# Second attention of a two-layer model on one core: values of four heads in one step, long VectorE steps apart from one another, fronts begun earlier, stores issued later

## The chip, the cores and the metric

The kernel runs on one core of a Trainium2 chip. The metric is the time of one execution on the device in microseconds; of several runs the median counts. The profiler recorded one further execution, and all durations below are from that one.

## What is computed

The reference is a model of two layers over 16 x 512 = 8192 tokens of width 128, all in f32. Layer 0 (a recurrence, an attention and a ternary feed-forward) is not touched by the change. Layer 1 is `x + attention(xn) + experts(xn)`, with `xn` the normed `x`. Its attention has 16 heads of width 64. Queries see keys in a window of their own 128 positions and the 128 before, and besides 32 "global" keys, one for each segment of 16 positions, made by a softmax pooling of the segment. Cut to what matters:

```
q, kv  = rotary(x @ Wq) * SCALE, rotary(x @ Wkv)      # kv serves as keys and values
local  = layernorm(kv) of the block before and of this one
pkv    = softmax(segments(kv) @ Wproj)
glob   = layernorm(sum(segments(kv) * pkv))
sim    = [q . glob , q . local]  (masked)
attn   = softmax(sim);   o = attn @ [glob, local];   out = o @ Wout + bout
```

The experts take each token to one of 8 (the largest of a softmax, at most 1024 tokens each), run two matmuls with a relu between, and add the result scaled by the probability.

## The kernel before, in words

Layer 0 takes the first 5650 us of the span. Then comes the part named here the second stage. It handles 64 **units** of 128 positions (four to a sequence; t = 0 is the first of a sequence and has no block before it). A unit has four **groups** of four heads, so there are 256 groups, and the loop over `i` at the end of the kernel (lines 1477 to 1492) takes one group a turn.

Each group has three pieces, called by hand in this loop. `scores` (L1328) multiplies queries and keys into four PSUM tiles, has VectorE add the mask and take the maximum (L1350, written to `pr` and `am`) and ScalarE take the exponential (L1351). `weights_by_key` (L1359) transposes `pr` on TensorE in two halves of two heads each (tiles `pp`, L1373), and once per group the 32 global weights (`gp`, L1366), which VectorE copies to `gt` (L1368). `values` (L1378) multiplies the transposed weights with values into `o`; it too is called for two heads at a time. The loop runs `scores(i)`, then `weights_by_key(i-1, 0)`, `values(i-2, 0)`, `weights_by_key(i-1, 1)`, `values(i-2, 1)`. The tiles of `scores`, `gp` and `pp` share a ring of five PSUM buffers, so that each of them waits until the one five places ahead has been read. All else (projections, transposes of the fronts, experts) shares a ring of two, named `m_...`.

Between these pieces the loop calls `work(1)` six times a group (so 24 times a unit). `work` (L1446) walks through a list of generators, in a fixed order of rank, and runs each whose time has come up to its next `yield`. A `yield` with a positive n means "come back in n steps, and I have used this step's turn"; a negative one only sets the delay, and others may still run; 0 means "ask me again at the next step". The generators are

- `back(u)` (L1407), the end of unit u: the inverse of the softmax sum (`sum`, `rd`), stored and loaded again broadcast over partitions (`rb`), `ot = ot * rb` on GpSimd (L1430), the output projection `m_po` (L1435, L1436), a store to `r_d`.
- `front(u)` (L1159), the start of unit u: load `xu`, matmuls `m_kv` and `m_q`, rotary (GpSimd L1186 `raw`, L1189/1190 `kv`, L1208 `qt`), the norm's sums on VectorE (L1211 `hm`, L1213 `hd`, L1222 `hv`, L1234 `pl`) with `by_w` on GpSimd (L1217), the normed `n` (L1243) and its transposes (`m_nt`), pooling (`m_gp`), `gm`, `gd`, `gr`, then `lk` and `gv` on GpSimd (L1297 to L1304), and a store and loads that spread the global values into `gvb`.
- `routing()`: the router, then 64 scatters of tokens to the experts by GpSimd (`xe_d`), then 16 expert halves (`m_xep`, `m_hp`, `m_yp`).
- `results()` (L1127): after the experts, for each of 64 blocks a gather by GpSimd (`gy`), a load of `r_d`, the sum on VectorE (`res`, L1146) and the store of the output.

Each engine runs what it is given strictly in the order in which the program issues it; there is no scheduler behind. So the order is set by the loop, the ranks and the yields. A store or load stands in SyncE's queue, and one that waits holds those behind it. I name a place by group and step: 1.2 is the second `work` call in the second group of a unit (groups 0 to 3, steps 1 to 6).

Of the kernel before, what the change touches and what calls it, by code (L numbers as in the profile page):

```python
# [23 lines left out]
NT = T // P  # L24
# [45 lines left out]
def tile_kernel(  # L70
# [868 lines left out]
    with (  # L939
# [59 lines left out]
        def routing():  # L999
# [75 lines left out]
            xts = {}  # L1075
            for t in range(NT + 3):
                if t < NT:
                    xts[t] = wk.tile([P, D], F32, name=f"xts_{t}", tag="xts", bufs=4)
                    nc.sync.dma_start(xts[t], xt_d[t * P : (t + 1) * P, :])
                if t >= 3:  # L1080
                    nc.gpsimd.indirect_dma_start(
                        out=xe_d,
                        out_offset=bass.IndirectOffsetOnAxis(ap=slot[:, t - 3 : t - 2], axis=0),
                        in_=xts.pop(t - 3),
                        in_offset=None,
                    )
                yield -2
# [7 lines left out]
        def expert_half(e, hf):  # L1095
# [10 lines left out]
            nc.sync.dma_start(xe, xe_d[at : at + S, :].rearrange("(t p) d -> p t d", p=P))  # L1106
            yield -3
            ps = misc(f"xep_{nm}")
# [6 lines left out]
            for f in range(4):  # L1115
                hp = misc(f"hp_{nm}_{f}")
                mm(hp, w1_sb[:, f * P : (f + 1) * P], xeT)
                nc.scalar.activation(he[:, f, :], hp, AF.Relu)
                yield 1 + f // 3
            yp = misc(f"yp_{nm}")  # L1120
# [8 lines left out]
        def results():  # L1129

            while not experts_done[0]:
                yield 0
            for t in range(NT):
                while stored[0] <= t:
                    yield 0
                gy = wk.tile([P, D], F32, name=f"gy_{t}", tag="gy", bufs=3)
                nc.gpsimd.indirect_dma_start(
                    out=gy,
                    out_offset=None,
                    in_=ye_d,  # L1140
                    in_offset=bass.IndirectOffsetOnAxis(ap=slot[:, t : t + 1], axis=0),
                )
# [3 lines left out]
                nc.vector.scalar_tensor_tensor(res, gy, pk[:, t : t + 1], res, ALU.mult, ALU.add)  # L1146
                nc.sync.dma_start(out[t * P : (t + 1) * P, :], res)

# [6 lines left out]
        units, groups = {}, {}  # L1155

        def front(u):

            U = units[u] = Unit()  # L1159
            U.normed = False  # L1160
# [28 lines left out]
            nc.gpsimd.tensor_tensor(k[:, :, 0, :], c_[:, :, 0, :], s_[:, :, 1, :], ALU.subtract)  # L1189
            nc.gpsimd.tensor_tensor(k[:, :, 1, :], c_[:, :, 1, :], s_[:, :, 0, :], ALU.add)  # L1190
            U.qt = wk.tile([P, NHP, P], F32, name=f"qt_{u}", tag="qt", bufs=3)
            for c in range(2):
# [15 lines left out]
                nc.gpsimd.tensor_tensor(U.qt[:, 4 * c : 4 * c + 4, :], parts[0], parts[1], ALU.add)  # L1208
# [4 lines left out]
            nc.vector.scalar_tensor_tensor(  # L1213
# [39 lines left out]
            nc.vector.reciprocal(ss, ss)  # L1253
            nc.gpsimd.tensor_tensor(se, se, ss.unsqueeze(2).broadcast_to(shape), ALU.mult)
            U.lk = lks[u % 4]
            for c in range(2):
                ps = misc(f"nt_{u}_{c}")
# [69 lines left out]
        def scores(i):  # L1327
# [26 lines left out]
            G.pg = wk.tile([P, 4, NSEG], F32, name=f"pg_{i}", tag="pg", bufs=2)  # L1354
            nc.scalar.copy(G.pg, pr[:, :, W:KW])
            if g == 3:
                streams.insert(0, [back(u), tick[0] + 2])

# [18 lines left out]

        def values(i, two):  # L1378

            u, g = divmod(i, 4)  # L1380
            U, G = units[u], groups[i]
            b, t = divmod(u, TB)
            w = 2 * (g % 2) + two
            if w == 0:
                U.o = ps_o.tile([P, 4, P], F32, name=f"o_{i}", tag="o")
            o = U.o[:, w, :]
            mm(o, gvbs[b % 2][:, g, 2 * two : 2 * two + 2, :].rearrange("p a d -> p (a d)"), G.gt, True, False)
            before = [u - 1, u] if t else [u]
            for c, k in enumerate(before):
                for a in range(2):  # L1390
                    mm(
                        o[64 * a : 64 * a + 64, :],
                        lks[k % 4][:, 4 * g + 2 * two + a, :],
                        G.pts[two][:, a, c, :],
                        False,
                        c == len(before) - 1,
                    )
            if two == 1:
                del groups[i]
            if w < 3:  # L1400
# [4 lines left out]
            U.done = g == 3  # L1405

        def back(u):  # L1407
# [3 lines left out]
            nc.vector.reciprocal(U.sum, U.sum)  # L1411
            yield -2
# [4 lines left out]
            yield 2  # L1417
            nc.sync.dma_start(rd_d[u % 2], rd)
# [11 lines left out]
            nc.gpsimd.tensor_tensor(U.ot, U.ot, rb, ALU.mult)  # L1430
            yield -4
            po = misc(f"po_{u}")
# [4 lines left out]
            nc.vector.tensor_tensor(res, po[:, 0:D], bout_row, ALU.add)  # L1437
            yield 2
            nc.sync.dma_start(r_d[u * P : (u + 1) * P, :], res)
# [3 lines left out]
        streams = []  # L1443
        tick = [0]

        def work(n):  # L1446

            for st in list(streams):
                if st[1] <= tick[0]:
# [8 lines left out]
            tick[0] += 1  # L1458

        NU = NT  # L1460
# [140 lines left out]
```

## Time and profile before

| what | value |
|---|---|
| median of 3 runs | 7826.6 us (7825.79 to 7835.86) |
| the profiled execution's own time | 7828.71 us |
| its span, first to last instruction | 7826.9 us |
| busy share of the span | PE 90%, DVE 61%, ACT 59%, POOL 38% |
| granted TensorE clock, mean | 0.938 of full speed |
| second stage in the span | from 5651.8 us (first `m_kv`) to the end |
| first and last `ot` product (L1430) | 5741.4 and 7814.1 us |

PE is TensorE, DVE VectorE, ACT ScalarE, POOL GpSimd, SP SyncE. In a row of groups the columns are: line, engine, operation, names of output and inputs, shapes, how often; after the bar busy time in us and the mean of one in ns; after the second bar the engine's idle time ahead of them and what ended it. A row of the timeline has the start in us, the duration in us, engine, line, operation, names, shapes and how many instructions were merged; an idle time in front of it stands in brackets. Each f32 matmul leaves two matmul records, transposes leave one. A matmul's form is the part of the array that it uses: 128*64 has a stationary operand of 64 columns, half the array's width.

The starts of the 64 `ot` products give the length of each unit. They fall in four stretches, by what runs besides fronts, groups and backs:

| units (intervals between `ot` products) | beside them | us per unit |
|---|---|---|
| 2 to 10 | scatters, 7 a unit | 33.4 |
| 11 to 26 | experts, one half a unit | 36.2 |
| 27 to 36 | gathers, 4 to 5 a unit | 35.6 |
| 37 to 59 | gathers, 1 a unit | 30.2 |

### The profile page before, as it was taken

What the parts mean: (1) busy time and instruction counts of PE and PEld (TensorE: products, weight loads), DVE (VectorE), ACT (ScalarE), POOL (GpSimd) and SP (SyncE); (2) the same over time, 40 slices, a digit from 0 to 9 for tenths busy, and PEclk for the clock granted to TensorE, in tenths of its full rate; (3) what the DMA queues carried; (4) which work ended last, traced back from release to release, by engine and by line L of the source; (5) the groups of instructions that cost most, each with busy time, mean ns of one, the idle gap of its engine ahead of it and who ended that gap; (6) DMA issues with size and microseconds to landing.
All of it is one profiled execution on the core that took longest, in us unless ns stands there. A gap on an engine that the chain in (4) does not pass through costs nothing. (4 is left out here: it accounts for less than half of the span.)

```text
span 7826.9 us, 107889 instructions
## 1 busy us (share of the span) xinstructions
PE 7010.5 (90%) x38168; PEld 3230.2 (41%) x38168; DVE 4782.5 (61%) x9622; ACT 4616.3 (59%) x9357; POOL 3012.6 (38%) x3763
## 2 busy tenths in 40 slices
PE   6898999999999999999999999999678999889898
PEld 2233333333333333333333333333256666666666
DVE  4565666566666666666666666666266555666665
ACT  3565655566555666656666666656355666556666
POOL 3333332232323233222222222222268655667775
PEclk7999999999999999999999999999789999989999
DMA  2221222212222221122211222222211111111111
GB/s 70 80 81 66 74 69 66 85 62 68 69 71 69 70 66 65 63 67 70 71 60 62 69 79 71 81 74 88 83 28 52 51 41 46 42 44 34 33 35 36
DMA packets 394780, 492.23 MB, mean 63 GB/s; under 512 B 82304, under 2 KB 278016, under 8 KB 393088
## 3 DMA queue, kind: packets, MB, share of 16 engines
q1 hardware_dynamic: 390144, 476.94, 19.5%
q0 software_dynamic: 4096, 8.40, 0.4%
q8 instruction: 302, 4.95, 0.3%
q14 instruction: 238, 1.95, 0.1%
HBM read 348.87 MB, written 133.17 MB: 62 GB/s over the span
## 5 line engine op out<-in xcount | busy, mean ns | idle before, releaser
L915 DVE TENSOR_REDUCE nm<-n 128x1 f32<-128x512 f32 x4096 | 2587.5, 682 | 1479.6 <-PE n L177 1477.9
L917 ACT ACTIVATE pt<-t 128x512 f32<-128x512 f32 x4096 | 2216.3, 595 | 1882.1 <-PE t L177 1857.4
L177 PE MATMUL n<-kt,qt 72*128 72x512 bf16 x4096 | 1323.5, 389 | 203.5 <-DVE nm L915 158.9
L177 PE MATMUL t<-qt,kt 75*128 75x512 bf16 x4096 | 1357.9, 391 | 104.1 <-ACT pt L917 56.0
L177 PE MATMUL o<-pt,vt 128*32 128x512 f32 x8192 | 1123.0, 671 | 0.0
L177 PEld LDWEIGHTS <-qt 72*128 72x128 bf16 x4096 | 354.7, 98 | 1026.3 <-issue 881.9
L177 PEld LDWEIGHTS <-kt 75*128 75x128 bf16 x4096 | 399.9, 99 | 849.8 <-issue 519.8
L1351 ACT ACTIVATE pr<-pr,am 128x288 f32<-128x288 f32 (+1 forms) x1024 | 508.0, 498 | 209.8 <-DVE am L1350 209.2
L867 POOL CAST nmp<-nm 128x16 bf16<-128x16 f32 x256 | 50.0, 195 | 1451.3 <-DVE nm L915 1451.3
L177 PEld LDWEIGHTS o<-pt,vt 128*32 128x32 f32 x8192 | 231.0, 118 | 661.1 <-issue 526.0
L467 POOL TENSOR_TENSOR qk<-qk,parts 128x512 f32<-128x512 f32 x128 | 147.9, 1155 | 769.3 <-ACT parts L280 739.7
L1350 DVE CUSTOM_DVE_ANT_0 pr<-s,cst 128x288 f32<-128x288 f32 (+1 forms) x1024 | 372.6, 419 | 44.5 <-PE s L994 44.1
L1373 PE MATMUL pp<-ident,pr 128*128 128x128 f32 x1792 | 311.5, 294 | 94.5 <-DVE am L1350 93.6
L994 PE MATMUL o<-pt,lk 128*64 128x128 f32 x3584 | 327.3, 300 | 0.0
L1375 ACT COPY pt<-pp 128x512 f32<-128x512 f32 (+1 forms) x512 | 264.9, 526 | 97.4 <-PE pp L1373 95.8
L1200 DVE TENSOR_TENSOR q<-m_q,cst 128x512 f32<-128x512 f32 x256 | 177.1, 692 | 220.1 <-PE m_q L994 220.1
L994 PE MATMUL s<-lkt,qt 64*128 64x288 f32 (+1 forms) x2048 | 298.3, 408 | 0.4 <-ACT lkt L1317 0.4
L177 PE MATMUL m_in<-x,w 128*128 128x512 f32 x512 | 279.6, 632 | 17.9 <-POOL x L330 9.7
L1373 PEld LDWEIGHTS pp<-ident,pr 128*128 128x128 f32 x1792 | 214.8, 148 | 162.9 <-DVE am L1350 130.2
L994 PE MATMUL m_q<-xu,wq_sb 128*128 128x128 f32 x2048 | 278.5, 279 | 1.9 <-ACT raw L1183 0.8
L177 PE MATMUL m_f<-n,w 128*128 128x512 f32 x512 | 274.0, 618 | 2.9 <-POOL n L330 2.6
L994 PEld LDWEIGHTS m_q<-xu,wq_sb 128*128 128x128 f32 x2048 | 249.4, 192 | 20.1 <-ACT raw L1183 16.0
(333 smaller groups left out, 11104.7 us busy)
## 6 DMA issues: line engine op xcount, KB each, us to landing
qt<-q_d SPq DMA_DIRECT2D x768, 96.0 KB
kt<-k_d SPq DMA_DIRECT2D x256, 288.0 KB
rb_n<-rstd_d SPq DMA_DIRECT2D x64, 512.0 KB
rb<-rd SPq DMA_DIRECT2D x128, 256.0 KB
q_d<-parts SPq DMA_DIRECT2D x64, 384.0 KB
k_d<-parts SPq DMA_DIRECT2D x64, 384.0 KB
o_d<-og SPq DMA_DIRECT2D x512, 36.0 KB
oa<-o_d SPq DMA_DIRECT2D x64, 256.0 KB
```

The costliest lines, as they stand in the source:

```text
L177: nc.tensor.matmul(out, lhsT=lhsT, rhs=rhs, start=first, stop=last)
L467: nc.gpsimd.tensor_tensor(x, x, parts[:, 0], ALU.subtract)
L867: nc.gpsimd.tensor_copy(parts[:, 0], nm)
L915: nc.vector.tensor_reduce(dst, n, AX.X, ALU.max, negate=True)
L917: nc.scalar.activation(dst, n, AF.Exp)
L994: nc.tensor.matmul(out, lhsT=lhsT, rhs=rhs, start=first, stop=last)
L1200: nc.vector.tensor_tensor(q, ps.rearrange("p (i t) -> p i t", t=P), const(name)[:, t * P : (t + 1) * P].unsqueeze(1).broadcast_to([P, 4, P ...
L1350: nc.vector.tensor_tensor_reduce(pr[:, j, 0:n], s[:, 0:n], mask(t), -1.0, BIG, ALU.add, ALU.min, nmax)
L1351: nc.scalar.activation(pr[:, j, 0:n], pr[:, j, 0:n], AF.Exp, bias=nmax, scale=-1.0, accum_out=U.sum[:, 4 * g + j : 4 * g + j + 1])
L1373: nc.tensor.transpose(pp[:, a, c, :], G.pr[:, 2 * two + a, at : at + P], ident)
L1375: nc.scalar.copy(pt[:, :, 0:n, :], pp[:, :, 0:n, :])
```

## The change

1. `values` is called once a group for all four heads, right after `scores`; and the product with the global weights `gt`, which was one matmul of 128 columns for two heads, becomes two of 64 columns each.
2. The front is pulled apart: `hm` and `hd`, `n` and the sums stand in steps of their own; a helper `quiet` keeps the front's long VectorE steps out of the last two steps of a group. The two waits for the previous front (`normed`, and a new `weighed`) stand before parts of the front instead of at its start; two counters, `scored` and `valued`, hold it back where buffers would be lacking.
3. A front begins two groups earlier (twelve steps).
4. Delays grow: a unit's `rd` store, the `m_po` product after `ot`, the `r_d` store, the store and loads of the global values, the loads of the experts' input, and the store of the output after `res`. The scatter of a block follows its load after two turns instead of three.

The six `work` calls of a group stay, in other places. No operation is taken out; 512 matmuls are added (two of 64 columns for each one of 128).

```diff
-            for t in range(NT + 3):
+            for t in range(NT + 2):
...
-                if t >= 3:
+                if t >= 2:
...
             xe = wk.tile([P, TB, D], F32, name=f"xe_{nm}", tag="x3", bufs=1)
             nc.sync.dma_start(xe, xe_d[at : at + S, :].rearrange("(t p) d -> p t d", p=P))
-            yield -3
+            yield -5
...
-                yield 1 + f // 3
+                yield 1 + f // 3 * 2
...
                 nc.vector.scalar_tensor_tensor(res, gy, pk[:, t : t + 1], res, ALU.mult, ALU.add)
+                yield -4
                 nc.sync.dma_start(out[t * P : (t + 1) * P, :], res)
...
+        def quiet():
+
+            while phase[0] in (4, 5):
+                yield 0
+
         def front(u):
...
-            while u - 1 in units and not units[u - 1].normed:
-                yield 0
             x = wk.tile([P, P], F32, name=f"xu_{u}", tag="xu", bufs=3)
             nc.sync.dma_start(x, x3_d[b][:, t * P : (t + 1) * P])
-            yield -3
+            yield -5
+
+            while u - 1 in units and not units[u - 1].weighed:
+                yield 0
...
+            while scored[0] < u - 2:
+                yield 0
             U.qt = wk.tile([P, NHP, P], F32, name=f"qt_{u}", tag="qt", bufs=3)
...
             yield -1
+            yield from quiet()
             mean = wk.tile([P, H1], F32, name=f"hm_{u}", tag="hm")
             nc.vector.tensor_reduce(mean, kv, AX.X, ALU.add)
+            yield -1
+            while u - 1 in units and not units[u - 1].normed:
+                yield 0
+            yield from quiet()
             d = wk.tile(heads, F32, name=f"hd_{u}", tag="hd", bufs=1)
...
             yield -2
+            yield from quiet()
             var = wk.tile([P, H1], F32, name=f"hv_{u}", tag="hv")
...
+            yield -1
+            yield from quiet()
             pl = wk.tile([P, H1], F32, name=f"pl_{u}", tag="pl")
             nc.vector.tensor_reduce(pl, by_w, AX.X, ALU.add)
-            yield -4
+            U.weighed = True
+            yield -2
...
-            n = wk.tile(heads, F32, name=f"n_{u}", tag="hq", bufs=1)
-            nc.vector.tensor_tensor(n, d, rstd.unsqueeze(2).broadcast_to(heads), ALU.mult)
...
             nc.scalar.activation(se, se, AF.Exp)
+            yield 1
+            yield from quiet()
+            n = wk.tile(heads, F32, name=f"n_{u}", tag="hq", bufs=1)
+            nc.vector.tensor_tensor(n, d, rstd.unsqueeze(2).broadcast_to(heads), ALU.mult)
             U.normed = True
-            yield 2
...
+            while valued[0] < u - 2:
+                yield 0
             lk = U.lk
...
             yield -5
-            nc.sync.dma_start(gv_d[u % 2], gv[:, 0, :])
             ps = misc(f"gkt_{u}")
...
             yield -2
+            nc.sync.dma_start(gv_d[u % 2], gv[:, 0, :])
+            yield -4
             src = gv_d[u % 2].rearrange("(g j s) d -> j s g d", j=4, s=n_seg)
...
-                streams.insert(0, [back(u), tick[0] + 2])
+                streams.insert(0, [back(u), tick[0] + 3])
...
-        def values(i, two):
+        def values(i):
...
-            mm(o, gvbs[b % 2][:, g, 2 * two : 2 * two + 2, :].rearrange("p a d -> p (a d)"), G.gt, True, False)
...
+            for two in range(2):
+                o = U.o[:, 2 * (g % 2) + two, :]
+                for c, k in enumerate([None] + blocks):
+                    for a in range(2):
+                        if k is None:
+                            v, w = gvbs[b % 2][:, g, 2 * two + a, :], G.gt
+                        else:
+                            v, w = lks[k % 4][:, 4 * g + 2 * two + a, :], G.pts[two][:, a, c - 1, :]
+                        mm(o[64 * a : 64 * a + 64, :], v, w, c == 0, c == len(blocks))
...
             nc.gpsimd.tensor_tensor(U.ot, U.ot, rb, ALU.mult)
-            yield -4
+            yield -6
...
-            if i % 4 == 0 and begun[0] < NU:
+            if (i == 0 or i % 4 == 2) and begun[0] < NU:
                 begin()
...
                 scores(i)
+                phase[0] = 0
                 work(1)
+            if i >= 2:
+                values(i - 2)
+            work(1)
             for two in range(2):
                 if 0 <= i - 1 < NG1:
                     weights_by_key(i - 1, two)
-                    work(1)
-                if i >= 2:
-                    values(i - 2, two)
-                    work(1)
+                work(1)
+            work(1)
             work(1)
```

Left out are the counters' own lines, the delays of `back` (2 to 3, 2 to 5, 2 to 5) and unchanged code.

More of the change, by code (lines that the diff above doesn't have):

```diff
@@ L1079, in routing @@
                     nc.sync.dma_start(xts[t], xt_d[t * P : (t + 1) * P, :])
-                if t >= 3:
+                if t >= 2:
                     nc.gpsimd.indirect_dma_start(
                         out=xe_d,
-                        out_offset=bass.IndirectOffsetOnAxis(ap=slot[:, t - 3 : t - 2], axis=0),
-                        in_=xts.pop(t - 3),
+                        out_offset=bass.IndirectOffsetOnAxis(ap=slot[:, t - 2 : t - 1], axis=0),
+                        in_=xts.pop(t - 2),
                         in_offset=None,
@@ L1155, in tile_kernel @@
         units, groups = {}, {}
+        def quiet():
+            while phase[0] in (4, 5):
+                yield 0
         def front(u):
             U = units[u] = Unit()
-            U.normed = False
+            U.normed = U.weighed = False
             b, t = divmod(u, TB)
-            while u - 1 in units and not units[u - 1].normed:
-                yield 0
             x = wk.tile([P, P], F32, name=f"xu_{u}", tag="xu", bufs=3)
             nc.sync.dma_start(x, x3_d[b][:, t * P : (t + 1) * P])
-            yield -3
+            yield -5
+            while u - 1 in units and not units[u - 1].weighed:
+                yield 0
             pair = [P, H1, 2, 32]
@@ L1255, in front @@
             U.lk = lks[u % 4]
+            yield -2
             for c in range(2):
@@ L1355, in scores @@
             nc.scalar.copy(G.pg, pr[:, :, W:KW])
+            scored[0] += g == 3
             if g == 3:
-                streams.insert(0, [back(u), tick[0] + 2])
+                streams.insert(0, [back(u), tick[0] + 3])
         def weights_by_key(i, two):
@@ L1376, in weights_by_key @@
             G.pts.append(pt)
-        def values(i, two):
+        def values(i):
             u, g = divmod(i, 4)
-            U, G = units[u], groups[i]
+            U, G = units[u], groups.pop(i)
             b, t = divmod(u, TB)
-            w = 2 * (g % 2) + two
-            if w == 0:
+            if g % 2 == 0:
                 U.o = ps_o.tile([P, 4, P], F32, name=f"o_{i}", tag="o")
-            o = U.o[:, w, :]
-            mm(o, gvbs[b % 2][:, g, 2 * two : 2 * two + 2, :].rearrange("p a d -> p (a d)"), G.gt, True, False)
[L1388 to L1400, printed above, removed]
+            blocks = [u - 1, u] if t else [u]
+            for two in range(2):
[7 more added lines that the diff above has]
+                        mm(o[64 * a : 64 * a + 64, :], v, w, c == 0, c == len(blocks))
+            if g % 2 == 0:
                 return
@@ L1405, in values @@
             U.done = g == 3
+            valued[0] += U.done
         def back(u):
@@ L1411, in back @@
             nc.vector.reciprocal(U.sum, U.sum)
-            yield -2
+            yield -3
             ps = misc(f"rd_{u}")
@@ L1416, in back @@
             nc.vector.tensor_copy(rd, ps[0:H1, 0:P])
-            yield 2
+            yield 5
             nc.sync.dma_start(rd_d[u % 2], rd)
@@ L1437, in back @@
             nc.vector.tensor_tensor(res, po[:, 0:D], bout_row, ALU.add)
-            yield 2
+            yield 5
             nc.sync.dma_start(r_d[u * P : (u + 1) * P, :], res)
@@ L1444, in tile_kernel @@
         tick = [0]
+        scored = [0]
+        valued = [0]
+        phase = [0]
         def work(n):
@@ L1458, in work @@
             tick[0] += 1
+            phase[0] += 1
         NU = NT
```

## The prediction

> **What bounds the kernel now.** I read the busy shares by stretch first, then TensorE's waits over the second stage, then the timelines of PE, DVE and POOL. Only the second stage changes. Rows by stretch (start:end, length, busy us of PE, PEld, DVE, ACT, POOL, then clock, DMA share, GB/s):
>
> ```profile
> 7100.00:7700.00 600.00, 540.89 (x4650) 405.81 (x4650) 400.20 (x1190) 384.59 (x1150) 432.13 (x395) 0.95 0.13 34
> 6302.00:6592.00 290.00, 272.90 (x2228) 199.59 (x2228) 165.81 (x483) 177.98 (x505) 165.21 (x153) 0.99 0.17 45
> 5888.00:6157.00 269.00, 228.74 (x1919) 170.14 (x1919) 164.24 (x474) 158.76 (x470) 213.13 (x200) 0.94 0.19 52
> ```
>
> With experts PE is busy 94% at a clock of 0.99; with scatters POOL reaches 79%; in the plain stretch PE has 90% at 0.95. No engine is full everywhere. What PE waits for, 5700 us to the end (total us, times, longest):
>
> ```profile
> PE pp L1373 <- DVE am L1350: 93.6, 48, 6.8
> PE m_po L994 <- POOL ot L1430: 66.7, 56, 3.8
> PE o L994 <- DMA gvb<-gv: 33.3, 8, 5.2
> ```
>
> So PE waits 265 us in all, mostly for VectorE to read the scores (whose PSUM buffers `pp` takes over) and for GpSimd's `ot`.
>
> **Values.** Four heads before: one half of `values`, then what follows; a unit's first block has two half-width matmuls less:
>
> ```profile
> 7444.49 0.39 PE L994 MATMUL o<-gt,gvb 128*128 128x128 f32 x2
> 7444.81 0.66 PE L994 MATMUL o<-pt,lk 128*64 128x128 f32 x8
> 7445.40 1.16 PE L994 MATMUL m_q<-xu,wq_sb 128*128 128x128 f32 x8
> ...
> 5706.71 0.44 PE L994 MATMUL o<-pt,lk 128*64 128x128 f32 x4
> 5707.08 2.05 PE L994 MATMUL m_q<-xu,wq_sb 128*128 128x128 f32 x16
> ```
>
> From start to next start: 0.32 us for the full matmul, 0.59 for four halves, 0.37 for two. Two more halves thus cost 0.22, as much as a full one (`m_q`: 0.90 for four, 0.22 each); the remaining 0.10 ahead and 0.15 behind is the change of width. Two calls cost 2 x 0.91 = 1.81 us a group. After: 12 halves, 6 x 0.215, and one change of width, 0.24: 1.53 us. The Trainium skill, TensorEngine Tiling (Array Packing), Key Properties, says that a change of tiling mode, though not of the tile, drains TensorE; that agrees in sign with the 0.25. The same page, Instruction Overhead, speaks against the change: each matmul costs some 60 cycles however small, so splitting a full one buys nothing by itself. By it alone (a half priced as a full one, 0.22) the step would be 12 x 0.22 + 0.24 = 2.9 us, 1.1 us dearer a group; the row of two more halves for 0.22 denies that, since halves of different columns overlap. Bounds: 1.45 (no change of width counted) to 1.75 (12 x 0.146, the mean of four halves). I take 1.53, by the marginal row: 1.1 us less PE a unit. Adding up a unit's rows (scores 1.17, half of `pp` 0.44, `m_q` 0.95, `m_kv` 0.96, `m_po` 2.1 and so on) PE needs 25.8 us before and 24.8 after for t > 0, 5.2 less for t = 0; an expert half adds 8.3 (0.6 + 4 x 1.0 + 3.7).
>
> **Waits that go.** `values` now stands between `scores` and `pp`, giving VectorE 1.5 us more, and no long front step is right ahead of `scores`: the 93.6 us and the slow clock after them I count as gone. The load of `gvb` gets some 6 us instead of 1: the 33.3 go. What is late next is GpSimd.
>
> **Where GpSimd's queue is moved.** In the changed issue order a unit's GpSimd work runs `gr`, `lk` (0.2), `qt`, `gd`, `gv`, `qt` (0.5), a gather or scatter (0.5), `by_w` (1.2), `ot` (1.4), and `m_po` comes at 2.4. Before, `raw` and both `kv` stood where now the second `qt`, a gather or scatter and `by_w` stand ahead of `ot`, and `m_po` was late by only 0.7 to 1.4 us. These rows bear on it (POOL, DVE, PE):
>
> ```profile
> 7453.73 2.26 POOL L1208 TENSOR_TENSOR qt<-q,q 128x512 f32<-128x512 f32 x1
> ...
> 6734.97 2.35 POOL L1430 TENSOR_TENSOR ot<-ot,rb 128x1024 f32<-128x1024 f32 x1
> ...
> 6749.34 1.03 POOL L1137 DMA_INDIRECT gy<-ye_d,slot  x1 [0.15 <-issue]
> ```
> ```profile
> 7453.53 1.33 DVE L1213 SCALAR_TENSOR_TENSOR hd<-hm,kv 128x1024 f32<-128x1024 f32 x1
> ...
> 6735.49 1.98 DVE L1146 SCALAR_TENSOR_TENSOR res<-gy,pk,res 128x128 f32<-128x128 f32 x1
> ...
> 6752.05 0.35 DVE L1146 SCALAR_TENSOR_TENSOR res<-gy,pk,res 128x128 f32<-128x128 f32 x1 [1.61 <-DMA gy<-ye_d,slot]
> ```
> ```profile
> 6740.31 0.77 PE L994 MATMUL o<-gt,gvb 128*128 128x128 f32 x2 [5.15 <-DMA gvb<-gv]
> ```
>
> `qt` takes 1.23 alone and 2.26 beside `hd`; `res` takes 0.34 alone and 1.98 beside `ot`, ending as `ot` ends. So the two exclude each other. The skill, GPSIMD Engine Reference, Specifications, only says that VectorE instructions with two SBUF inputs contend with GpSimd for the interfaces; by that rule without the row I would have charged nothing definite, by the row it is the whole overlap, 1.2 us a unit for `hd`. A gather lands 2.7 us after its start (6749.34 to 6752.05). After the 5.15 us idle PE ran at half speed for four groups of rows: 0.69, 1.06, 0.90 and 2.53 us against 0.32, 0.59, 0.44 and 1.89, 1.9 us lost.
>
> **Units with gathers** (28 of them with two, since `results` now waits 3 + 4 steps a block and is last in rank; before, 4 to 5 a unit in ten units and then one). From the start of group 0's scores: scores 1.17, `rd` 0.15, values 1.53, `m_gp` 0.58: 3.43. `gr` starts 1.5 later (7438.86 to 7440.36): 4.9. Then 0.86 + 2.31 + 1.23 + 0.85 + 1.23 + 1.2 (`hd`): 12.6; the gather starts at 12.8 and lands at 15.5, `by_w` holds the port until 16.3, `res` (placed at 1.2 in VectorE's queue) ends at 16.6, `gt` of this unit's group 0 behind it at 16.85. Queued behind `res` are that `gt`, `hv`, and the maxima of group 2. PE by its own rows reaches group 2's third score matmul, whose buffer that `gt` frees, at 3.43 + 0.55 + 0.95 + 0.44 + 0.95 + 1.17 + 1.53 + 0.55 + 0.17 + 0.44 + 0.57 = 10.75. It waits 6.1 us. From there to the unit's end: 0.58 + 1.53 + 0.55 + 0.17 + 0.44 + 2.1 + 0.96 + 1.17 + 0.96 + 5.6 = 14.1. Sum 30.9, with 2.0 for the clock and 0.3 for gaps 33.2; t = 0 saves 2.9; mean 32.5. Bounds of this wait: 4.5 us if `res` is not late and only `ot` (done at 18.5, `m_po` due at 14.0) is, about 8 if `pl` and `m_plt` come late too.
>
> **Units with experts.** Experts' matmuls now stand at 0.5 to 2.2, in the very stretch in which PE would wait: `m_po` is due at 14.0 + 8.3 = 22.3, `ot` is done at 12.6 + 2.35 + 2.33 = 17.3. PE bounds: 24.8 + 8.3 + 0.8 (a wait for `he`'s buffer, gaps) = 33.9 to 34.2, t = 0 29.5: mean 33.0 against 36.2. This is the gain; its cover gone (a scarcer PE cover, `he` late by one more step), it costs up to 1 us a unit.
>
> **Units with scatters.** Two scatters lie ahead of `by_w` (1.2, and 2.5 with its wait for the one before, as in rows of 1.5 us idle): `ot` ends at 21.0, PE waits 7.0, then 10.8 to the end: 31.8 + 2.3 = 34.1, t = 0 32.2: 33.7 against 33.4.
>
> **Other edits.** Stores issued later are covered by buffers that have a group to spare; what each would cost uncovered is one landing, some 2 us. `xu` and the experts' inputs are loaded two steps sooner: nothing. `rb` is now issued one step before `ot`, but SyncE isn't held by steps: `rd` is copied at 2.4, two landings later, by 8, `rb` is there, and `ot` is due at 16: nothing. SyncE's `out` store waits for `res` and holds `xu` and `gvb` behind it until 16.6; these are needed at 25: nothing. Filling: group 0's scores now stand behind the second front's transposes (5697.7 instead of 5684.5), but the third front's projections are done by then: +5, between -10 and +20.
>
> **Sum**, first to last `ot`, 2072.7 us before. After: first two units 75, 10 x 33.7 = 337, 17 x 33.0 = 561, 28 x 32.5 = 910, 3 x 32.5 = 98, last three 63: 2044, thus -29; with filling -24. From the profiled execution's 7828.7: 7805; the median lies 2.1 below: 7803.
>
> **Rivals.**
> *The gather's wait decides (slower).* Place: `res` at 1.2 on VectorE, behind a gather behind six GpSimd steps, in 28 units. Price as above 6.1 us; each further us a unit costs 28. It turns the sign at 32.5 + 24/28 = 33.4 us a unit. For it: the units with gathers before took 35.6, with a 5.15 us idle among them; against: they had twice the gathers. At 35.0: 7873.
> *GpSimd keeps ahead (much faster).* If `lk` or the gather slip in between, only `ot` is late: 31.0 a unit with gathers and 32 with scatters: 7803 - 28 x 1.5 - 10 x 1.7 = 7744. For it: `gr` might be ready earlier; against: the queue is strict and its rows are steady.
> *The change does not do what it says.* If halves don't overlap so well (1.75), three of four `values` lie on the path of each unit: 64 x 0.66 = +42: 7845.
>
> **Numbers.** A measurement of this kernel tells 0.2% (16 us) from no change. My likeliest case, 0.42, has its own range 7770 to 7835 and is split: 0.22 faster, 0.17 within, 0.03 slower. GpSimd ahead: 0.25, faster. The gather's wait: 0.25, of it 0.22 slower. Halves: 0.08, slower. So faster 0.47, within 0.20, slower 0.33. Two in ten are left out by 7720 to 7880.
>
> **What would show it.** Right: expert units at 33, a group of `o` rows in 1.5 us, no `pp` waiting for `am`; in units with gathers one idle of 6 us on PE in group 2, ended by `gt` or `am`, with `res` waiting for `gy` on VectorE. Wrong: `m_po` or nothing waiting there; expert units still at 36; an idle elsewhere, at `m_plt` or `m_nt`.

## The result and the profile after

The changed kernel takes 7932.7 us (median of 4 runs, 7924.4 to 7939.5) against 7826.2 us of before (4 runs): ratio 1.0132, 95% interval 1.0119 to 1.0145. It is slower by 106 us, where 7803 us had been forecast, and outside the forecast's 7720 to 7880 us. The profiled execution took 7929.1 us with a span of 7927.1 us at a granted TensorE clock of 0.929. The difference lies wholly in the second stage.

Unit lengths, measured as before by the starts of the `ot` products:

| intervals between `ot` products | beside them | forecast, us per unit | measured |
|---|---|---|---|
| first `ot` | | at 5746 | at 5746.9 |
| 0 and 1 | | 75 in all | 75.2 in all |
| 2 to 11 | scatters | 33.7 | 35.0 |
| 12 to 28 | experts | 33.0 | 34.2 |
| 29 to 56 | two gathers a unit | 32.5 | 35.5 |
| 57 to 59 | one gather a unit | 32.5 | 34.9 |
| the last three | | 63 in all | 63.3 in all |

10 x 1.3 + 17 x 1.2 + 28 x 3.0 + 3 x 2.4 is 125 us: that is the whole miss, 7929 less 7805. Two thirds of it lie in the units with gathers. The busy time by stretch, scatters, experts and two gathers (columns as before: PE, PEld, DVE, ACT, POOL, then the clock, DMA share, GB/s):

```profile
5822.00:6172.00 350.00, 269.39 (x2444) 208.48 (x2445) 194.65 (x582) 189.81 (x571) 263.99 (x248) 0.91 0.17 47
6230.00:6753.00 523.00, 483.34 (x4494) 367.93 (x4493) 317.50 (x918) 334.85 (x965) 319.88 (x295) 1.00 0.18 47
6754.00:7746.00 992.00, 742.54 (x7000) 577.14 (x7000) 644.89 (x1709) 542.39 (x1624) 636.59 (x588) 0.87 0.13 35
```

With gathers TensorE is busy 75% of the stretch at a clock of 0.87; in the plain units of before it was 90% at 0.95. What it waits for over the second stage, and what VectorE's `res` waits for:

```profile
PE s L994 <- DVE gt L1391: 209.8, 33, 7.1
PE m_gkt L1330 <- POOL gv L1325: 66.3, 45, 5.7
PE m_plt L1257 <- DVE pl L1250: 50.1, 14, 5.5
PE m_q L994 <- DVE sw L1296: 46.0, 59, 0.8
PE m_hp L994 <- ACT he L1118: 14.7, 13, 1.4
...
PE o L994 <- DMA gvb<-gv: 9.3, 9, 1.5
PE m_po L994 <- POOL ot L1449: 8.2, 7, 6.6
...
DVE res L1146 <- DMA gy<-ye_d,slot: 136.6, 32, 5.2
```

The old waits are gone or small: `pp` for `am` from 93.6 to 2.4 us, `m_po` for `ot` from 66.7 to 8.2, `o` for `gvb` from 33.3 to 9.3. A new one stands at the very place that the prediction named, TensorE's third score matmul of group 2 behind `gt`, in all 28 units with two gathers: 180.7 of the 209.8 us are theirs.

The values step, four heads at once, is even a little cheaper than forecast, 1.46 us from 7520.16 to 7521.62:

```profile
7520.16 0.44 PE L994 MATMUL o<-gt,gvb 128*64 128x128 f32 x4
7520.43 0.61 PE L994 MATMUL o<-pt,lk 128*64 128x128 f32 x8
7520.86 0.39 PE L994 MATMUL o<-gt,gvb 128*64 128x128 f32 x4
7521.08 0.61 PE L994 MATMUL o<-pt,lk 128*64 128x128 f32 x8
7521.62 0.65 PE L994 MATMUL m_gp<-kv,sw 128*32 128x64 f32 x32
```

The same unit around its gather, the rows of POOL, then DVE, then PE:

```profile
7531.38 1.10 POOL L1137 DMA_INDIRECT gy<-ye_d,slot  x1 [0.16 <-issue]
7532.51 2.34 POOL L1230 TENSOR_TENSOR by_w<-kv,rows_sb 128x1024 f32<-128x1024 f32 x1
7534.81 2.33 POOL L1449 TENSOR_TENSOR ot<-ot,rb 128x1024 f32<-128x1024 f32 x1
...
7533.99 3.32 DVE L1146 SCALAR_TENSOR_TENSOR res<-gy,pk,res 128x128 f32<-128x128 f32 x1 [4.70 <-DMA gy<-ye_d,slot]
7537.23 0.28 DVE L1391 COPY gt<-gp 128x128 f32<-128x128 f32 x1
...
7537.56 0.91 PE L994 MATMUL s<-lkt,qt 64*128 64x160 f32 x4 [5.43 <-DVE gt L1391]
```

The gather lands 2.6 us after its start (2.7 had been forecast), and `res` begins in the middle of `by_w`. But `res` does not end with `by_w` at 7534.85. It goes on until `ot` ends: 7533.99 + 3.32 = 7537.31, against 7537.14. A step of 0.34 us took 3.32. In the units with two gathers the `res` at 2.5 took 0.34 us each time, the one at 1.2 between 2.8 and 3.4. `gt`, in the queue behind it, came 2 us later than reckoned.

### The profile page after: what moved, and what is told of

Its sections match the earlier page's. It is cut to its first block, busy times and chain, and to the rows that moved or that the text cites. A ratio compares the mean times of both kernels' runs of the same rounds, so it can differ in the third digit from the quotient of the medians.

```text
span 7927.1 us, 109846 instructions
## 1 busy us (share of the span) xinstructions
PE 6923.7 (87%) x39192; PEld 3217.7 (41%) x39192; DVE 4851.8 (61%) x9622; ACT 4609.6 (58%) x9357; POOL 3018.8 (38%) x3763
## 5 line engine op out<-in xcount | busy, mean ns | idle before, releaser
L994 PE MATMUL s<-lkt,qt 64*128 64x288 f32 (+1 forms) x2048 | 333.2, 429 | 216.4 <-DVE gt L1391 209.8
L994 PEld LDWEIGHTS s<-lkt,qt 64*128 64x128 f32 x2048 | 182.5, 196 | 337.1 <-DVE gt L1391 225.5
L994 PE MATMUL o<-pt,lk 128*64 128x128 f32 x3584 | 311.1, 291 | 0.1
L1396 PE MATMUL pp<-ident,pr 128*128 128x128 f32 x1792 | 291.3, 284 | 2.4 <-DVE am L1372 2.4
```

Of the source, the lines that this page charges most:

```text
L994: nc.tensor.matmul(out, lhsT=lhsT, rhs=rhs, start=first, stop=last)
L1396: nc.tensor.transpose(pp[:, a, c, :], G.pr[:, 2 * two + a, at : at + P], ident)
```

## The experiments

Where one GpSimd step follows another without a gap, the point between them is called a seam here. Theory A: `res` at 1.2 sets the unit, because of the gather's landing and because GpSimd's `by_w` and `ot` keep it out beyond the seam between them; `gt` stands behind it. Rivals: the number of gathers or the later stores; the matmuls of 64 columns; the length of GpSimd's chain by itself. Each ratio is to the kernel before, run on the same chip, with its 95% interval.

### e1: `res` one block later

```diff
-    nc.vector.scalar_tensor_tensor(res, gy, pk[:, t : t + 1], res, ALU.mult, ALU.add)
+    if last:
+        pr_, pg_ = last
+        nc.vector.scalar_tensor_tensor(pr_, pg_, pk[:, t - 1 : t], pr_, ALU.mult, ALU.add)
     yield -4
-    nc.sync.dma_start(out[t * P : (t + 1) * P, :], res)
+    if last:
+        nc.sync.dma_start(out[(t - 1) * P : t * P, :], pr_)
+    last = (res, gy)
...
```

> The changed kernel, but each `res` step of results() works on the block gathered one turn before, at the same step as now (1.2 and 2.5). Instructions, steps and number of gathers stay. Theory A (VectorE, waiting at 1.2 for a gather that stands behind GpSimd's queue, and then locked out by `by_w` and `ot`, costs the 28 units with two gathers their time): these units fall from 35.5 to about 31, bound by `ot` alone, and the kernel to about 7805 us, the `res` rows to under 2 us each. Theory B (the longer GpSimd chain ahead of `m_po` sets the time in any case, the wait of VectorE only hides it): units at 33.5 or more, PE waits at `m_po` instead, kernel at 7875 or above. Theory C (sw, lkt and the clock): hardly any change, 7925.

Measured: 7776.5 us, ratio 0.9923 (0.9903 to 0.9943). Units with two gathers 30.7 us, TensorE's clock in them 0.96. No `res` waits for `gy`; at 1.2 it takes between 0.34 and 1.36 us. What TensorE still waits for:

```profile
PE m_plt L1265 <- DVE pl L1258: 95.6, 46, 5.8
PE m_gkt L1338 <- POOL gv L1333: 67.1, 45, 6.1
...
PE s L994 <- DVE gt L1399: 20.1, 16, 3.5
```

The wait for `gt` fell from 209.8 to 20.1 us, and of that `m_plt`, the next late one, took 45 back. The number of gathers and their places are unchanged, so these alone are not the cause. The rest of the change gains: without this one wait it is faster than before. This edit removes both halves of theory A at once, `res`'s wait for its gather and the keeping out; e11 removes only the second.

### e2: the output's store right behind `res`

```diff
                 nc.vector.scalar_tensor_tensor(res, gy, pk[:, t : t + 1], res, ALU.mult, ALU.add)
-                yield -4
                 nc.sync.dma_start(out[t * P : (t + 1) * P, :], res)
```

> The changed kernel without the new delay between `res` and its store, so that results() catches up in eight units with four or five gathers each and then needs one a unit, but with `res` still at 1.2 right behind its gather at 0.5. Theory A: the wait is there in every unit, whatever the number of gathers: units 38 to 59 stay at 35, the kernel moves by less than 15 us from 7933 (the eight units may be longer, 38). Theory D (the 28 units of two gathers instead of one are what costs, by GpSimd's added time): units 38 to 59 fall to 31 to 32, the kernel to about 7860.

Measured: 8001.9 us, ratio 1.0208 (1.0182 to 1.0235). Neither theory's number. With one gather a unit the units (37 to 56) took 36.7 us, not 30 or 32: the gather and its `res` stand at the same bad places, and a second wait came in:

```profile
PE s L994 <- DVE gt L1390: 129.6, 33, 4.8
PE m_po L994 <- POOL ot L1448: 80.5, 39, 6.3
```

The store, now at 1.2, waits for `res` on SyncE, and the load of `rb`, issued at 1.3, stands behind it; over the second stage GpSimd's `ot` waited 178.5 us in 30 places for `rb`, against 20.2 in 3 in the changed kernel. So the later store, which I had priced at nothing, keeps this wait away.

### e3: the kernel before with only this later store

```diff
                 nc.vector.scalar_tensor_tensor(res, gy, pk[:, t : t + 1], res, ALU.mult, ALU.add)
+                yield -4
                 nc.sync.dma_start(out[t * P : (t + 1) * P, :], res)
```

> The kernel before, with only the delay of four steps between `res` and its store added: gathers spread at two a unit over 26 units. Theory A: at the places that the order before gives them (gather at 2.1 with `res` at 2.5, gather at 3.4 with `res` at 0.3) a gather costs one to two us a unit: units of two gathers at 32, kernel within 25 us of 7826. Theory D: these units rise to 35 and the kernel to 7890.

Measured: 7835.2 us, ratio 0.9997 (0.9986 to 1.0009). Two gathers a unit, at the places of before, make units of 32.4 us, against 30.1 in this kernel's units with one. So at those places two gathers cost a little over 2 us a unit, not 5.

### e4: the changed kernel with `gt` at full width

```diff
-                for c, k in enumerate([None] + blocks):
+                mm(o, gvbs[b % 2][:, g, 2 * two : 2 * two + 2, :].rearrange("p a d -> p (a d)"), G.gt, True, False)
+                for c, k in enumerate(blocks):
...
-                        if k is None:
-                            v, w = gvbs[b % 2][:, g, 2 * two + a, :], G.gt
...
```

> The changed kernel with the product of the global weights as one matmul of 128 columns again (all else stays, four heads in one step). By the prediction's rows a group's values take 1.8 us instead of 1.46 to 1.53. Theory A: on the path of every unit, so expert units (PE bound) rise by 1.1 to 1.4 us, units with gathers by about 1, the kernel by 40 to 60 us to about 7980. If the change of width costs nothing beside other work: no change, 7933.

Measured: 8000.5 us, ratio 1.021 (1.0188 to 1.0232). Units with experts, where TensorE is the bound, went from 34.2 to 35.3, those with gathers lost 1.3 and those with scatters 0.8. That the first is the 1.1 us a unit of the prediction is in part luck: the values step itself went from 1.46 to 1.90 us a group (6401.98 to 6403.88), more than the 1.8 reckoned, and shorter waits took some of it back (`m_gkt` from 66.3 to 37.1 us, `m_hp` from 14.7 to 10.7).

### e6: the kernel before with only this split

```diff
-            mm(o, gvbs[b % 2][:, g, 2 * two : 2 * two + 2, :].rearrange("p a d -> p (a d)"), G.gt, True, False)
+            for a in range(2):
+                mm(o[64 * a : 64 * a + 64, :], gvbs[b % 2][:, g, 2 * two + a, :], G.gt, True, False)
```

> The kernel before, with only the product with the global weights split into two matmuls of 64 columns; still two calls of values a group, at their places. Theory A (a change of width costs 0.25 us in all, and what the change saves is one of two such pairs a group; split alone, each call still has its pair, 3 x 0.215 + 0.24 = 0.885 us instead of 0.91): within 15 us of before, 7825. Theory B (the halves are what saves, as far as the 67 us say that the run with full width lost against the changed kernel): about -60, 7775. Theory C (every matmul has a fixed price, as the page on array packing says, and 512 more of them cost it): slower, by up to 64 x 8 x 0.07 = 36 us.

Measured: 7798.9 us, ratio 0.9967 (0.9953 to 0.9981): a gain of about 26 us, between theories A and B, and the opposite of C. One call of `values`, from its start to the next piece's:

```profile
7441.96 0.44 PE L994 MATMUL o<-gt,gvb 128*64 128x128 f32 x4
7442.23 0.61 PE L994 MATMUL o<-pt,lk 128*64 128x128 f32 x8
7442.77 0.65 PE L1373 MATMUL pp<-ident,pr 128*128 128x128 f32 x4
```

0.81 us instead of 0.91. So a group costs 1.82 us before, 1.62 with the split, and 1.46 with the split in one step: the larger part is the split itself, not the saved change of width, contrary to theory A. One step without the split costs 1.90 (e4) and gains nothing; there the width changes as often as before.

### e5: the kernel before with part 1 alone

```diff
                 scores(i)
...
+            if i >= 2:
+                values(i - 2)
+            work(1)
             for two in range(2):
                 if 0 <= i - 1 < NG1:
                     weights_by_key(i - 1, two)
-                    work(1)
-                if i >= 2:
-                    values(i - 2, two)
-                    work(1)
+                work(1)
+            work(1)
             work(1)
```

> The kernel before, with part 1 of the change alone: the values of four heads in one step right after the scores, the product with the global weights in halves of 64 columns; fronts, delays, the place of the gathers as before. Theory A (the values step is worth what the rows priced: 1.81 to 1.5 us a group, 1.1 us of TensorE a unit, and the wait of pp for am goes): about -70 for the matmuls and up to -60 for the wait, some of it taken back by m_po, which already waits for GpSimd's ot: 7745, between 7710 and 7785; units with experts near 34.5. Theory B (the step's gain exists only on TensorE, every unit's end is set by GpSimd's ot): within 20 us of before, the waits m_po<-ot and m_q<-xu or the like growing by what values saves.

Measured: 8096.3 us, ratio 1.0345 (1.0317 to 1.0372), wrong for both theories. Every stretch is longer, the plain units 35.9 instead of 30.2 us. From 5700 us on TensorE's idle time grew by 223 us (487 against 264), its busy time by 34 at a clock of 0.89 instead of 0.95:

```profile
PE m_po L994 <- POOL ot L1425: 117.7, 64, 3.4
PE m_nt L1261 <- DVE se L1247: 80.5, 62, 1.4
...
PE o L994 <- ACT pt L1375: 52.9, 43, 1.7
PE m_rd L1409 <- DVE sum L1406: 52.8, 52, 2.5
```

Before, these stood at 66.7, 28.1, none listed and 3.0. In the issue order a half of `values`, 0.91 us of TensorE, stood between `ot` and `m_po`, between `se` and `m_nt`, and between the inverse of the sum and `m_rd`. With part 1 alone it is gone from all three places, and the delays between producer and user, counted in steps, are as short as before. That fits the size (52.8 us over the 64 `m_rd`, 0.8 each), but it is not shown by a run of its own. By itself part 1 doesn't pay; which of parts 2 to 4 makes up for it was not tested.

### e8: the changed kernel, `lk` moved

```diff
             nc.gpsimd.tensor_tensor(gr, gr, neg_half[:, 0:1], ALU.pow)
-            nc.gpsimd.tensor_tensor(lk, lk, row(2).unsqueeze(1).broadcast_to(heads), ALU.add)
...
             yield -2
+            nc.gpsimd.tensor_tensor(lk, lk, row(2).unsqueeze(1).broadcast_to(heads), ALU.add)
             nc.sync.dma_start(gv_d[u % 2], gv[:, 0, :])
```

> The changed kernel with only GpSimd's second lk step moved from 0.2 to 1.6; res stays at 1.2 behind a gather of the same unit. Theory A (the gather starts where six GpSimd steps have ended, and res, gt and the third score matmul of group 2 come by as much earlier as the chain is shorter): the wait for gt falls by 2.2 us a unit, units with gathers from 35.5 to about 33.2, those with scatters by 1 to 2: 7840, between 7815 and 7870. Theory B (the wait is set by something else than this chain, say the landing of the gather in a loaded DMA queue, or the clock): above 7900.

Measured: 7865.1 us, ratio 1.0034 (1.0022 to 1.0047). Units with gathers 33.3 us: theory A's size. But the cause of what remains changed: the mean `res` in the stretch with gathers fell to 0.51 us, and the mean `hd` rose from 1.3 to 3.8. e7 shows how.

In half of these units (16) `res` stands exactly as in the changed kernel, 1.5 us into `by_w` with `ot` behind it at a seam, and yet it gets in at that seam. POOL, then DVE:

```profile
7500.03 2.34 POOL L1230 TENSOR_TENSOR by_w<-kv,rows_sb 128x1024 f32<-128x1024 f32 x1
7502.34 2.41 POOL L1449 TENSOR_TENSOR ot<-ot,rb 128x1024 f32<-128x1024 f32 x1
...
7498.91 1.24 DVE L1226 SCALAR_TENSOR_TENSOR hd<-hm,kv 128x1024 f32<-128x1024 f32 x1
...
7501.55 0.98 DVE L1146 SCALAR_TENSOR_TENSOR res<-gy,pk,res 128x128 f32<-128x128 f32 x1 [1.39 <-DMA gy<-ye_d,slot]
```

`res` ends 0.16 us after `by_w`, where in the changed kernel it ended 0.17 after `ot`. So a seam alone does not keep VectorE out. What differs in the rows is ahead of it: here `hd` still runs when `by_w` begins, and there VectorE had been idle since `hd`.

### e7: e1 with `lk` moved

The edit is e1's and e8's together.

> The changed kernel with res one block later (as in the first experiment, 7776.5), and with GpSimd's second lk step (2.35 us, ahead of qt, gd and gv in its queue) moved from 0.2 to 1.6, just ahead of the store of gv. Theory A (what is left on TensorE's path is the length of GpSimd's chain from gr over qt, gd, gv to by_w and ot, which ends in m_gkt<-gv, m_plt<-pl and part of m_po<-ot): these waits, 67 + 96 + 18 us, fall to under 40 us together, units with gathers from 30.7 to about 29.3, with scatters from 34.7 to about 33: 7690, between 7660 and 7720. Theory B (these waits only stand in for something else, such as VectorE's own queue): above 7750, with the same us in other waits.

Measured: 7839.4 us, ratio 1.0008 (0.9998 to 1.0018), 0.9% slower than e1 where 1% faster had been expected. `m_gkt` and `m_plt` hardly wait any more (2.7 and 12.4 us), as theory A had it, but `s` waits 120.7 us for `gt` again. POOL, then DVE, then PE:

```profile
7531.05 1.10 POOL L1138 DMA_INDIRECT gy<-ye_d,slot  x1 [0.17 <-issue]
7532.18 2.34 POOL L1238 TENSOR_TENSOR by_w<-kv,rows_sb 128x1024 f32<-128x1024 f32 x1
7534.48 2.33 POOL L1457 TENSOR_TENSOR ot<-ot,rb 128x1024 f32<-128x1024 f32 x1
...
7531.68 6.22 DVE L1234 SCALAR_TENSOR_TENSOR hd<-hm,kv 128x1024 f32<-128x1024 f32 x1
7538.09 0.28 DVE L1399 COPY gt<-gp 128x128 f32<-128x128 f32 x1
...
7532.00 0.76 PE L994 MATMUL s<-lkt,qt 64*128 64x288 f32 x4
7538.42 2.42 PE L994 MATMUL s<-lkt,qt 64*128 64x288 f32 x4 [5.66 <-DVE gt L1399]
```

With GpSimd 2.35 us earlier, another VectorE step now meets `by_w` and `ot`: `hd`, with two inputs in SBUF as well, takes 6.22 us instead of 1.22, in 16 of the 32 units in which a gather stands right ahead of `by_w`. In the other 16 it begins 0.9 or 1.1 us ahead of `by_w` and takes 1.23, and `res`, which begins 0.05 to 0.2 us into `by_w`, gets in at the seam and takes 2.4. The units are 35 us long in the first case and 29 to 30 in the second. The last two rows show what an idle time costs behind it: the same two score matmuls take 0.76 us before it and 2.42 after it.

### e10: e7 with `by_w` held until `hd` is done

```diff
             by_w = wk.tile(heads, F32, name=f"by_w_{u}", tag="raw", bufs=1)
+            seen = wk.tile([P, 1], F32, name=f"seen_{u}", tag="seen")
+            nc.gpsimd.tensor_scalar(seen, d[:, 0, 0:1], 1.0, None, ALU.mult)
             nc.gpsimd.tensor_tensor(by_w, kv, row(0).unsqueeze(1).broadcast_to(heads), ALU.mult)
```

> The seventh experiment's kernel (res later, lk moved; 7839) with one wait more: a GpSimd step of one column, which reads hd, stands ahead of by_w. In the kernel of e7 hd took 6.22 us instead of 1.22 in every unit with gathers, from the gather on through by_w and ot, and gt waited behind it on VectorE. Theory A (hd is kept out by GpSimd's by_w and ot, which follow each other without a gap): by_w begins about 1 us later, hd takes 1.2 to 1.7 us, the wait of s for gt falls from 121 us to under 35, units with gathers from 32.4 to about 29.5, with experts from 35.2 to about 34.2: 7735, between 7690 and 7765. Theory B (hd is slow for another reason, the wait only costs): 7840 or more.

Measured: 7696.3 us, ratio 0.9832 (0.9803 to 0.9861), units with gathers 28.6 us, with experts 33.8, the wait for `gt` 24.0 us. POOL, then DVE:

```profile
7415.04 1.09 POOL L1138 DMA_INDIRECT gy<-ye_d,slot  x1 [0.17 <-issue]
7416.99 0.26 POOL L1239 TENSOR_SCALAR seen<-hd 128x1 f32<-128x1 f32 x1 [0.86 <-DVE hd L1234]
7417.23 2.35 POOL L1240 TENSOR_TENSOR by_w<-kv,rows_sb 128x1024 f32<-128x1024 f32 x1
7419.55 2.36 POOL L1459 TENSOR_TENSOR ot<-ot,rb 128x1024 f32<-128x1024 f32 x1
...
7415.66 1.23 DVE L1234 SCALAR_TENSOR_TENSOR hd<-hm,kv 128x1024 f32<-128x1024 f32 x1
```

A wait of 0.86 us and a step of 0.26 on GpSimd, added and nothing taken away, gained some 140 us against e7. `hd` begins 0.62 us after the gather's start, as in the row of e7 (0.63), but now `by_w` doesn't follow before it is done, and it takes 1.23 us instead of 6.22. (In e7 that held for half of the units, not for every one, as the expectation says.) This is the fastest kernel of the study, faster than before and after.

### e11: the changed kernel, `ot` held until `res` is done

```diff
...
+            if summed:
+                seen = wk.tile([P, 1], F32, name=f"seen_{u}", tag="seen")
+                nc.gpsimd.tensor_scalar(seen, summed.pop()[:, 0:1], 1.0, None, ALU.mult)
             nc.gpsimd.tensor_tensor(U.ot, U.ot, rb, ALU.mult)
```

(`summed` holds the last `res`.)

> The changed kernel with one wait more: a GpSimd step of one column, which reads the res just summed, stands ahead of ot. So GpSimd has a gap between by_w and ot in which res can run. Nothing else is moved. Theory A (res, landed at 2.6 us after the gather's start, is ready before by_w ends, and only by_w and ot in a row keep it until ot ends, 2.3 us more): res ends about 0.3 us after by_w, gt and the third score matmul of group 2 come 2 us earlier in the units with gathers, and ot 0.6 us later, which costs little: units with gathers 33.6 instead of 35.5: 7932 - 31 x 1.9 = 7873, between 7855 and 7895. Theory B (the wait for gt comes from the landing of gy alone, or from TensorE's clock): 7925 or more, since ot comes later.

Measured: 7874.4 us, ratio 1.0069 (1.0043 to 1.0095); units with gathers 33.4 us, theory A's numbers. The same rows as above of the changed kernel:

```profile
7413.35 2.34 POOL L1232 TENSOR_TENSOR by_w<-kv,rows_sb 128x1024 f32<-128x1024 f32 x1
7415.94 0.26 POOL L1453 TENSOR_SCALAR seen<-res 128x1 f32<-128x1 f32 x1 [0.25 <-DVE res L1146]
7416.17 2.35 POOL L1454 TENSOR_TENSOR ot<-ot,rb 128x1024 f32<-128x1024 f32 x1
...
7414.83 1.02 DVE L1146 SCALAR_TENSOR_TENSOR res<-gy,pk,res 128x128 f32<-128x128 f32 x1 [3.90 <-DMA gy<-ye_d,slot]
```

`by_w` ends at 7415.69 and `res` at 7415.85: with a gap behind `by_w`, `res` runs in it, as the prediction had assumed for the changed kernel, in all 32 units with such a gather. What TensorE then waits for `gt` and `m_gkt` in the 28 units is 109.6 + 37.8 us, 5.3 a unit. The kernel is still 0.7% slower than before: this step explains 2.1 x 28 = 59 of the 125 us of the miss.

### e9: `ot` in four pieces

```diff
-            nc.gpsimd.tensor_tensor(U.ot, U.ot, rb, ALU.mult)
+            for k in range(4):
+                nc.gpsimd.tensor_tensor(U.ot[:, 2 * k : 2 * k + 2, :], U.ot[:, 2 * k : 2 * k + 2, :], rb[:, 2 * k : 2 * k + 2, :], ALU.mult)
```

> The changed kernel with GpSimd's ot product, one instruction of 1024 columns and 2.33 us, split into four of 256 columns. It asks how res is kept out: in the changed kernel res lands before by_w ends, yet ends only when ot ends, 3.3 us instead of 0.34. Theory A (the lock is held for one instruction at a time, and res gets in between two of them): res ends at latest with the first quarter, some 0.7 us instead of 2.3 after by_w, gt and the third score matmul of group 2 come 1.6 us earlier, less than that where the four fixed costs lengthen ot by 0.2: about 7885, between 7870 and 7905. Theory B (a queue of GpSimd instructions without a gap keeps VectorE out to its end, whatever their size): the same as the changed kernel or a little slower, 7925 to 7950, res still at 3.2 us or more.

Measured: 7931.4 us, ratio 1.0124 (1.0101 to 1.0148), the same as the changed kernel. Rows of one unit, POOL and DVE in order of time:

```profile
7550.37 2.34 POOL L1230 TENSOR_TENSOR by_w<-kv,rows_sb 128x1024 f32<-128x1024 f32 x1
7551.82 3.07 DVE L1146 SCALAR_TENSOR_TENSOR res<-gy,pk,res 128x128 f32<-128x128 f32 x1 [4.68 <-DMA gy<-ye_d,slot]
7552.66 2.81 POOL L1450 TENSOR_TENSOR ot<-ot,rb 128x256 f32<-128x256 f32 x4
```

`res` stayed out over the end of `by_w` and over the first two seams of `ot`; it ended at 7554.89, 0.6 us before the last piece. So it was in all 32 such units. Smaller instructions gave VectorE no earlier turn worth having (theory B, but for the last seam); the gap of e11 did.

## Why the prediction was wrong, point by point

**The step that failed**: "`by_w` holds the port until 16.3, `res` (placed at 1.2 in VectorE's queue) ends at 16.6". I took the row of before in which `res` ends as `ot` ends and charged one GpSimd step. Here `ot` follows `by_w`, and `res` is kept out through both: 2.8 to 3.4 us, in all 32 units with a gather right ahead of `by_w`. e11 puts a gap there and gets the forecast end and 2.1 of the 3.0 us a unit back.

The row itself had been read rightly, and it had a seam too. This stood right behind its `ot` (6734.97 to 6737.32), and `res` got in at it and ended at 6737.47:

```profile
6737.28 1.31 POOL L1208 TENSOR_TENSOR qt<-q,q 128x512 f32<-128x512 f32 x1
```

In the kernel before, a `res` or `hd` that a GpSimd step held up got in at the seam behind it each time, 42 of 42. The step that failed was to carry this over to a pair that stands right behind a gather. Over all the kernels here, 237 of 237 such steps got in at the first seam where no gather stood right ahead of the GpSimd step that held them, even between `by_w` and `ot` (17 `hd` in e7, e8 and the changed kernel, in units without a gather). Right behind a gather it was 32 of 160, namely those of e7 and e8 in which `hd` still ran as `by_w` began. No run moves the gather away and leaves the rest, so why the seam is lost there stays open.

**The size of the wait.** Forecast 6.1 us a unit for `gt` in the units with gathers. Measured 180.7 / 28 = 6.5 for `gt`, 1.4 ahead of it for `m_gkt` behind `gv`, and elsewhere in the unit 0.8 for `m_q` behind `sw` and 0.2 for `m_pwp`: 8.9 in all. The time at `m_gkt` is taken off the wait for `gt`, so these two, 7.9 us, are the forecast 6.1 with the 2 us by which `res` is late; in e11, where it is not late, they are 5.3. `sw` and `m_pwp` I had not listed. The first cost 46.0 us over the stage, 0.8 in nearly every unit, in the fastest kernel (e10) too, and no run removes it. Busy time with the slow clock was 26.5 us a unit (742.5 / 28), 26.1 in the forecast.

**Rival 1 named the place and the mechanism's end**, with 35.0 us a unit and 7873 us. Its units came at 35.5; the rest of the 7929 are the units with scatters and experts. I had given it 0.25.

**Units with experts**: 34.2 instead of 33.0. The gain against 36.2 is real. The 0.8 us allowed for gaps was too small: 14.7 / 17 = 0.9 us for `m_hp` behind `he`, 0.8 for `sw`, 0.2 for `m_pwp`.

**Units with scatters**: 35.0 instead of 33.7. The wait of 7.0 us came, but in pieces and not at `m_po`: 43.9 us in ten units at `m_plt` behind `pl`, since `pl` needs `by_w` and `m_plt` stands ahead of `m_po` in TensorE's queue; 1.6 a unit more at `m_gkt`, 0.8 each at `sw` and `gvb`.

**Right**: the values step (1.53 forecast, 1.46), the waits that go, the filling, the last three units, nothing at `m_po` in the units with gathers. Of the 1.53 the split was undervalued (0.20 us a group by e6, where its expectation had 0.04) and the change of width overvalued (0.16, where 0.24 had been reckoned); that these two partly cancel is luck.

**Stores issued later, priced at nothing.** Right for the sum, since nothing waits for them. e2 shows what the later `out` store covers, some 60 us (ratio 1.0208 against 1.0132).

## What to carry to other kernels

For each VectorE step with two inputs in SBUF, list the GpSimd steps that may run beside it. Usually the end of the first one is what counts (237 of 237 here); where a gather on GpSimd stands right ahead of it, reckon to the first gap: a step of 0.34 us cost 3.3, one of 1.2 cost 6.2. Shortening a chain moves such a meeting to another step (e7), while a short wait on GpSimd, which lets VectorE go first, can gain (e10: some 140 us). A load's consumer that may be late does not belong ahead of a small copy on which the bound engine waits (e1: some 160 us).

## What the runs showed of the hardware

- VectorE can be kept out not for one GpSimd instruction but for a row of them: 3.3 us for `res` over two, 6.2 for `hd`, still 3.0 for `res` when one of the two was cut into four (e9). A gap of about 0.25 us was enough (e11). Each of these rows began right behind a gather. Elsewhere `res` and `hd` got in at the first seam and ended about 0.15 and 1.08 us behind it.
- It isn't certain even behind a gather: in half of the units of e7 and e8 `res` got in at the seam between `by_w` and `ot`. There `hd` had begun 0.02 or 0.2 us after the gather's start and still ran as `by_w` began; in the other half it began 0.63 us after the gather's start, 0.5 us ahead of `by_w`, and lost. What decides is open.
- The gather, an indirect DMA, does not by itself keep VectorE out: `hd` ran beside it in 1.23 us, begun at that same 0.62 us (e10). To lose, `hd` needs `by_w` behind it (e7).
- Splitting a matmul of 128 columns into two of 64 made the values call cheaper, 0.81 us against 0.91 (e6), though it has one matmul more for each split.
